# Selective-scan layer on one core: the low-order bfloat16 pieces of B formed by TensorE in PSUM instead of by GpSimd subtractions

## The chip, the cores and the metric

One core of one Trainium2 chip runs the whole program as one launch. The metric is the device time of a launch in microseconds. The kernel before took 12329.48 us, the median of three runs (12318.48, 12329.48 and 12333.17). A further run was profiled: it took 12328.75 us, of which 12326.7 us lie between its first and its last instruction.

## The reference, cut to what matters

Four layers run in sequence on x of shape (8, 64, 64, 64). Only the first, a vision state-space layer, is touched by the change. For each of 8 images, 128 channels d, 4 scan directions k and 16 states n it computes, along a sequence of 4096 pixels t:

```
x_dbl = einsum('bkdl,kcd->bkcl', xs, xproj_w)         # 4 + 16 + 16 rows: step sizes, B, C
dt    = softplus(dtproj(x_dbl[:4]) + dtproj_b)        # per channel d
h[d,n,t] = h[d,n,t-1] * exp(dt[d,t] * A[d,n]) + dt[d,t] * B[n,t] * u[d,t]
y[d,t]   = sum_n h[d,n,t] * C[n,t]
```

Directions 0 and 2 read the image by rows, forward and backward; 1 and 3 by columns. B[n,t] does not depend on the channel, so the kernel has to spread one row of B over 128 partitions for every state n.

## The kernel before, in words

**Units, steps and images.** `scan_layer` cuts a sequence into 4 chunks of `CH` = 1024 pixels. A chunk of one direction is a *step*, and a step has 16 *turns* n = 0 to 15, one for each state. Eight images of 16 steps make 2048 turns. Images 0 to 6 take the directions in the order 0, 2, 1, 3; the last image takes 1, 3, 0, 2. In this text step s = 0 is the first of the 16 steps of an image.

**What a turn does.** ScalarE writes a = exp(dt*A_n) (`decay`, L733). The row of B for the state is spread over the partitions in one of two ways: for n in `BY_POOL` = 0, 3, 6, 8 a broadcast DMA brings it as `bt`, GpSimd multiplies it by dt*u (`product`, L741) and ScalarE copies it to PSUM tile z (`spread`, L748); for the twelve other states TensorE spreads it into z with two 512-column bfloat16 matmuls against the 0/1 matrix `pick` (L751), and VectorE multiplies z by dt*u (L778). VectorE then runs the scan (`tensor_tensor_scan`, L782) into h, GpSimd multiplies h by the broadcast row of C (`ct`, L787), and TensorE adds the product into `yps` by an identity matmul (`sum_up`, L848), two to three turns later. h has three buffers, a three, z two, `ct` five and `bt` two.

**The three pieces of B.** The bfloat16 matmul would lose bits of B, so B is stored as three bfloat16 pieces stacked on 48 partitions, which `pick` adds up: p0 = bf16(B), p1 = bf16(B - p0), p2 = bf16(B - p0 - p1). The function `pieces` makes them once for each chunk and each pair of directions, that is in the step ahead of every step with k < 2. Its parts are hung on turns of the running step (`hooks`): `fetch` reads B (128x256 float32, tile `bw`) back from DRAM, `first` rounds it on ScalarE (L691), `subtract` forms the remainder `br` on GpSimd (L695), `second` rounds that on ScalarE (L698), `third` subtracts again on GpSimd (L701), `store` writes the three pieces with three DMAs (L706), and `get` reads them as `bs` (L713). In the general case these stand at turns 7, 8, 9, 10, 11, 12 and 13. For directions 2 and 3 only `get` is needed, at turn 13. I call the steps in which the pieces for the next step are made *parts steps*: 64 of the 128, four of which are at the start (made as the first image is being filled) and have another placement.

**What sets the order.** The order is written out by hand (`manual_schedule`): each engine runs its instructions strictly in program order. A queue of smaller items (`Background`: projections, normalization, convolution, output) gives one item to a turn, made by `bg.before` and finished by `bg.after` one turn later. In the turns listed in `idle` (6, 7, 8) only items without TensorE work may run. The two softplus activations of the next step stand at turns 6 and 7 (L653 and L656, the second with two table loads around it), its sum at turn 8 (L659), and dt*u of the next step at turn 11 (L678, GpSimd). At turn 3 `begin_sum` (L839) opens a new `yps` after ScalarE has emptied the last (L817).

**Normalization of y.** `norm_y` puts, among other items, eight `variance` items in the queue. Each one ends in `put`: ScalarE copies a row into `vrow` (L344), of which there is one buffer, and SyncE's queue sends it to DRAM (L345). Between some of the variance items stand items that only load (`load(at)`).

Of the kernel before, what the change touches and what calls it, by code (L numbers as in the profile page):

```python
# [11 lines left out]
BF16 = mybir.dt.bfloat16  # L12
AF = mybir.ActivationFunctionType
ALU = mybir.AluOpType
# [14 lines left out]
NCH = L // CH  # L29
# [212 lines left out]
def scan_layer(cm, x_in, w, xh):  # L242

    tc, nc = cm.tc, cm.nc
    with ExitStack() as ctx:
# [34 lines left out]
        for k in range(4):  # L280
# [5 lines left out]
            ps = psum.tile([128, BK], F32, name="wps", tag="mm")  # L286
# [31 lines left out]

        eps = cm.tile([128, 1], "eps")
        nc.vector.memset(eps, 1e-5)  # L320
        pick = cm.pool.tile([3 * N, N], BF16, name="pick", tag="pick")
        rows = work.tile([3 * N, N], F32, name="rows", tag="vsm")
        nc.vector.tensor_reduce(
# [7 lines left out]
        def bank(name):  # L331
            return psum.tile([128, BK], F32, name=name, tag="mm")
# [93 lines left out]
        def norm_y(y, blocks, load, multiply, project_out):  # L426

            put, chain, sm = inverse_root(len(blocks))
            j0, nb, sq = blocks[0], len(blocks), {}

            def square(j):
                sq[j] = work.tile([128, BK], F32, name="sq", tag="sq")
                nc.scalar.activation(sq[j], y[:, bass.ts(j, BK)], AF.Square)

            def variance(j):
                def make():
                    ps = bank("vps1")
                    nc.tensor.matmul(
                        ps[:1], lno_avg[:, NBK - 1 : NBK], sq.pop(j), start=True, stop=True
                    )  # L440
                    return ps

                def use(ps):
                    put(ps, 1, j - j0)
                    if j + 2 in blocks:
                        square(j + 2)

                return make, use

            def apply(j):  # L450
                def make():
                    ps = bank("rps")

                    row = cm.ident[:nb, j - j0 : j - j0 + 1].to_broadcast([nb, DI])
                    nc.tensor.matmul(ps, row, sm["r"], start=True, stop=True)
                    return ps

                def use(ps):
                    v = y[:, bass.ts(j, BK)]
                    nc.vector.tensor_tensor(v, v, ps, ALU.mult)  # L460
                    nc.scalar.activation(v, v, AF.Identity, bias=on_b, scale=on_g)
                    if j - 1 in blocks:
                        multiply(j - 1)

                return make, use

            out = [(None, lambda _: [square(j) for j in blocks[:2]]), none]
            for j in blocks:
                out.append(variance(j))
                if j in blocks[1:6:2] or nb == 2:  # L470
                    at = j if nb == 2 else j0 + (j - j0) // 2
                    out.append((None, lambda _, at=at: load(at)))
            out += chain
            out += [apply(j) for j in blocks[:2]]
            end = (None, lambda _: multiply(blocks[-1]))
            if nb == 2:
                out += [end, none]
            for j in blocks:
                if j + 2 in blocks:
                    out.append(apply(j + 2))  # L480
                    if j + 2 == blocks[-1]:
                        out.append(end)
                out += [project_out(j), none]
            return out
# [191 lines left out]
        def step_input(ctl):  # L676

            nc.gpsimd.tensor_tensor(ctl["dus"], ctl["dt"], ctl["ut"]["u"], ALU.mult)  # L678


        def pieces(ctl, low):

            by_place = "a n (j x) -> (n j) a x"

            def fetch():
                low["b"] = work.tile([128, 2, 128], F32, name="bw", tag="bw", bufs=1)
                nc.sync.dma_start(low["b"], low["bc"][:, :N].rearrange(by_place, x=128))

            def first():
                low["p"] = work.tile([128, 3, 2, 128], BF16, name="bp", tag="bp", bufs=1)  # L690
                nc.scalar.copy(low["p"][:, 0], low["b"])  # L691

            def subtract():
                low["r"] = work.tile([128, 2, 128], F32, name="br", tag="br", bufs=1)
                nc.gpsimd.tensor_tensor(low["r"], low["b"], low["p"][:, 0], ALU.subtract)  # L695

            def second():
                nc.scalar.copy(low["p"][:, 1], low["r"])  # L698

            def third():  # L700
                nc.gpsimd.tensor_tensor(low["p"][:, 2], low["r"], low["p"][:, 1], ALU.subtract)  # L701

            def store():
                low["bsd"] = dr.tile([2, 3 * N, CH], BF16, name="bsd", tag="bsd", bufs=8)
                for i in range(3):
                    nc.sync.dma_start(  # L706
                        low["bsd"][:, i * N : (i + 1) * N].rearrange(by_place, x=128),
                        low["p"][:, i],
                    )

            def get():
                ctl["bs"] = work.tile([3 * N, CH], BF16, name="bs", tag="bs")
                nc.sync.dma_start(ctl["bs"], low["bsd"][ctl["k"] // 2])  # L713

            return ([fetch, first, subtract, second, third, store] if ctl["k"] < 2 else []) + [get]


        BY_POOL = (0, 3, 6, 8)
# [5 lines left out]
        def load(ctl, n, t):  # L724

            bcr = ctl["bc"].rearrange("(t n) l -> t n l", t=2)
            name = "bt" if t == 0 else "ct"
            ctl[name, n] = bcp.tile([DI, CH], F32, name=name, tag=name, bufs=5 if t else 2)
            nc.sync.dma_start(ctl[name, n], bcr[t, n].unsqueeze(0).broadcast_to([DI, CH]))
# [128 lines left out]
        def steps(b):  # L858


            out = []
            for k in (0, 2, 1, 3) if b < NB - 1 else (1, 3, 0, 2):
                cs = range(NCH) if k < 2 else range(NCH - 1, -1, -1)
                out += [(k, c, i) for i, c in enumerate(cs)]
            return out
# [3 lines left out]
        def prepare(b, s):  # L869

            if b not in images:
                return None
            u = images[b]["u"]
            k, c, i = steps(b)[s]
            ks = [steps(b)[q * NCH][0] % 2 for q in range(4)] + [0]
            q = s // NCH
            bg.finish(b, 2 * c + 2 if s < NCH and k == 0 else NBK)
            low = lows.setdefault((b, k % 2, c), {}) if k < 2 else lows.pop((b, k % 2, c))
            dt, ut, e, items, soft = project(u, k, c, low)
            if b == 0 and s < NCH:  # L880
                items = later.pop(s, []) + items + [(None, soft[0]), (None, soft[1])]
            bg.add(items, first=True)
            new = work.tile([DI, N], F32, name="state", tag="state", bufs=3)
            ctl = dict(
                b=b, k=k, c=c, u=u, into=("row", "col")[ks[q + q % 2]], dt=dt, bc=low["bc"][k // 2], ut=ut, dus=e, soft=soft, new=new, state=None,
                first=(i == 0), new_y=(s < NCH), turns=(s % (2 * NCH) == NCH - 1),
                mat=lno_cen if s >= 3 * NCH - 1 else cm.ident,
            )
            ctl["pieces"] = pieces(ctl, low)
            return ctl  # L890


# [18 lines left out]
        with tc.manual_schedule():  # L911
            start(0)
            bg.drain()
            ctl = prepare(0, 0)
# [12 lines left out]
            for b in range(NB):  # L927
                for s in range(4 * NCH):


                    early, late = b == 0 and s + 1 < NCH, b == NB - 1 and s > 3 * NCH
                    if s + 1 < 4 * NCH:
                        nxt = prepare(b, s + 1)
                    else:
                        nxt = prepare(b + 1, 0)
                    bg.credit = 2 if b == NB - 2 else 1
                    idle = () if early or late else (6, 7, 8)
                    hooks = {}
                    if nxt:
                        do = nxt["pieces"]  # L940
                        if early:
                            hooks = {
                                12: [do[0]], 13: [nxt["soft"][2], lambda: step_input(nxt)] + do[1:5],
                                14: do[5:6], 15: do[6:],
                            }
                        else:
                            hooks = {14 - len(do) + i: [f] for i, f in enumerate(do)}
                            for i, f in zip((6, 7, 8), nxt["soft"]):
                                hooks[i] = hooks.get(i, []) + [f]
                            hooks[11] = hooks.get(11, []) + [lambda: step_input(nxt)]  # L950
# [51 lines left out]
                    ctl = nxt  # L1002
# [1155 lines left out]
```

## Time and profile before

| | |
|---|---|
| median of three runs | 12329.48 us |
| profiled execution | 12328.75 us, span 12326.7 us |
| TensorE busy | 11203.1 us (91%), 38827 matmul records |
| VectorE busy | 10359.2 us (84%) |
| ScalarE busy | 7820.8 us (63%) |
| GpSimd busy | 7399.3 us (60%) |
| scan layer | about 94 us to 7010 us of the span |
| GpSimd L695 and L701 | 43.1 and 43.2 us in all, 64 of each, 674 and 675 ns |
| ScalarE L691 and L698 | 25.6 and 25.9 us in all, 401 and 405 ns |

The busy shares are over the whole program. The scan layer fills a little over half of the span; the later layers hardly use GpSimd, so its share inside the scan layer is far higher than 60%. A time that a listing gives as "us" is the busy time of one instruction or of several merged ones ("x4"); the distance from one start to the next is often shorter than that, because the end of one overlaps the start of the next. An idle time is written in brackets with what ended it.

### The profile page before, as it was taken

The page shows a single profiled execution, that of the slowest core. Times are in us where ns is not written, and L with a number is a line of the kernel's source. Part 1 is how long each engine was busy: PE and PEld are TensorE (multiplying, and loading weights), DVE is VectorE, ACT ScalarE, POOL GpSimd, SP SyncE. Part 2 cuts the span into 40 slices and gives each one's busy share as a digit, 9 for nine tenths or more (in the row PEclk, how much of TensorE's full clock was granted, in tenths as well). Part 3 has the DMA queues.
Part 4 walks back from the last instruction along what each step waited for, and adds up shares of the span by engine and source line. Part 5 has one row for each costly group of instructions (what it writes and reads, how often), then busy time and mean ns, then how long its engine had stood idle before and what let it go on. Part 6 is the DMA issues. An engine that isn't in the chain of part 4 may idle for free. (4 is left out here: it accounts for less than half of the span.)

```text
span 12326.7 us, 120038 instructions
## 1 busy us (share of the span) xinstructions
PE 11203.1 (91%) x38827; PEld 4075.9 (33%) x38827; DVE 10359.2 (84%) x7334; ACT 7820.8 (63%) x10409; POOL 7399.3 (60%) x3510
## 2 busy tenths in 40 slices
PE   7899999999999999999998899999987779999999
PEld 2233332332332332333322233232335463333333
DVE  5999999999999999999999776868677686676767
ACT  4776776776766766767766554646547574555554
POOL 5999999999999999999999700000006480000000
PEclk8999999999999999999999899999998789999999
DMA  3666666666666666666666400000011100000000
GB/s 115 207 213 218 209 209 217 219 203 216 218 210 213 211 210 217 213 215 213 199 213 211 164 24 26 5 25 7 17 41 41 41 21 24 19 4 19 5 11 6
DMA packets 541331, 1562.16 MB, mean 127 GB/s; under 512 B 127360, under 2 KB 144400, under 8 KB 538128
## 3 DMA queue, kind: packets, MB, share of 16 engines
q1 hardware_dynamic: 540688, 1554.36, 38.5%
q8 instruction: 309, 5.06, 0.2%
q14 instruction: 334, 2.74, 0.1%
HBM read 1456.41 MB, written 88.87 MB: 125 GB/s over the span
## 5 line engine op out<-in xcount | busy, mean ns | idle before, releaser
L787 POOL TENSOR_TENSOR ct<-ct,h 128x1024 f32<-128x1024 f32 x2048 | 4794.6, 2364 | 248.2 <-DVE h L782 113.3
L782 DVE TENSOR_TENSOR_SCAN h<-a,state,z 128x1024 f32<-128x1024 f32 x1536 | 3573.1, 2342 | 118.2 <-ACT z L748 67.1
L1159 DVE TENSOR_TENSOR sum<-sum,ex 128x1024 f32<-128x1024 f32 x1920 | 2347.5, 1223 | 618.1 <-ACT ex L1152 484.4
L1152 ACT ACTIVATE ex<-sc 128x1024 f32<-128x1024 f32 x2048 | 1968.1, 1024 | 1359.6 <-PE sc L1147 1359.6
L848 PE MATMUL yps<-ct,ident 128*128 128x512 f32 x5632 | 2809.0, 630 | 2.5 <-POOL ct L787 2.4
L733 ACT ACTIVATE a<-dt,amat 128x1024 f32<-128x1024 f32 x2048 | 2345.4, 1147 | 725.9 <-DVE h L782 712.5
L778 DVE TENSOR_TENSOR z<-z,e 128x1024 f32<-128x1024 f32 x1536 | 1863.3, 1213 | 221.1 <-PE z L751 143.2
L1166 PE MATMUL av<-ex,v 128*64 128x512 f32 x8192 | 1950.0, 604 | 0.0
L1147 PE MATMUL sc<-q,k 16*128 16x512 f32 (+1 forms) x8192 | 1562.2, 623 | 4.2 <-ACT q L1140 3.1
L848 PEld LDWEIGHTS yps<-ct,ident 128*128 128x128 f32 x5632 | 1006.4, 194 | 1384.2 <-issue 1220.6
L751 PE MATMUL z<-bs,pick 48*128 48x512 bf16 x3072 | 948.0, 389 | 536.5 <-DVE h L782 485.5
L848 PE MATMUL yps<-ct,lno_cen 128*128 128x512 f32 x2560 | 1276.3, 630 | 0.0
L782 DVE TENSOR_TENSOR_SCAN h<-a,z 128x1024 f32<-128x1024 f32 x512 | 1162.7, 2282 | 81.4 <-ACT z L748 57.2
L741 POOL TENSOR_TENSOR bt<-bt,e 128x1024 f32<-128x1024 f32 x512 | 1210.1, 2364 | 5.3 <-DMA bt<-bc 5.3
L1473 POOL TENSOR_TENSOR gt<-gt,pad 128x1024 f32<-128x1024 f32 x16 | 34.9, 2179 | 1570.2 <-ACT gt L1472 1570.2
L1166 PEld LDWEIGHTS av<-ex,v 128*64 128x64 f32 x8192 | 512.2, 136 | 1332.8 <-issue 1278.9
L1147 PEld LDWEIGHTS sc<-q,k 16*128 16x128 f32 (+1 forms) x8192 | 528.4, 184 | 1016.2 <-issue 977.3
L748 ACT COPY z<-bt 128x1024 f32<-128x1024 f32 x512 | 519.8, 1015 | 537.5 <-POOL bt L741 334.8
L751 PEld LDWEIGHTS <-pick 48*128 48x128 bf16 x3072 | 177.6, 95 | 1754.9 <-DVE h L782 1003.0
L848 PEld LDWEIGHTS yps<-ct,lno_cen 128*128 128x128 f32 x2560 | 458.1, 193 | 618.3 <-issue 564.2
L544 PE MATMUL vps<-pad,convd 128*128 128x512 f32 x1152 | 550.9, 602 | 12.9 <-ACT e L648 12.9
L1846 DVE RECIPROCAL r<-e 128x512 f32<-128x512 f32 x128 | 420.7, 3323 | 0.0
(416 smaller groups left out, 10449.5 us busy)
## 6 DMA issues: line engine op xcount, KB each, us to landing
ct<-bc SPq DMA_DIRECT2D x2048, 512.0 KB
bt<-bc SPq DMA_DIRECT2D x512, 512.0 KB
x<-x SPq DMA_DIRECT2D x12, 2048.0 KB
bc<-e SPq DMA_DIRECT2D x128, 128.0 KB
zd<-z SPq DMA_DIRECT2D x64, 256.0 KB
z<-zd SPq DMA_DIRECT2D x64, 256.0 KB
x<-x SPq DMA_DIRECT2D x32, 512.0 KB
part<-x SPq DMA_DIRECT2D x128, 128.0 KB
```

What stands on the lines that cost most here:

```text
L544: nc.tensor.matmul(held[0].rearrange("p (r c) -> p r c", c=S), convd[:, t, :], pad[:, j * rows + dy : (j + 1) * rows + dy, dx : dx + S], s ...
L733: ctl["exp", n] = nc.scalar.activation(ctl["a", n], ctl["dt"], AF.Exp, scale=amat[:, ctl["k"], n : n + 1])
L741: nc.gpsimd.tensor_tensor(bt, bt, ctl["dus"], ALU.mult)
L751: nc.tensor.matmul(z[:, bass.ts(i, BK)], pick[:, n : n + 1].to_broadcast([3 * N, DI]), ctl["bs"][:, bass.ts(i, BK)], start=True, stop=True,)
L778: first = nc.vector.tensor_tensor(z, z, ctl["dus"], ALU.mult)
L782: nc.vector.tensor_tensor_scan(h[:, flip], a[:, flip], z[:, flip], 0.0 if state is None else state[:, n : n + 1], ALU.mult, ALU.add,)
L787: freed[at] = nc.gpsimd.tensor_tensor(ct, ct, h, ALU.mult)
L848: nc.tensor.matmul(ctl["ps"][:, bass.ts(i, BK)], ctl["mat"], ct[:, bass.ts(i, BK)], start=False, stop=(n == N - 1 and not ctl["turns"]),)
L1147: nc.tensor.matmul(sc[:, e, :], k[r : r + d, bass.ts(j, 128)], qs[i][r : r + d, :], start=True, stop=True,)
L1152: nc.scalar.activation(ex, sc, AF.Exp)
L1159: nc.vector.tensor_tensor(sums[i], sums[i], ex, ALU.add)
L1166: nc.tensor.matmul(avs[i][r, :], v[:, j, r], ex[:, e, :], start=(j == 0), stop=(j == TQ - 1))
```

## The change

`pieces` gets a second way to make p1 and p2, used everywhere but in the first four steps. `rest(i)` allocates a PSUM bank and lets TensorE form the remainder there: an identity matmul of the float32 B (256 columns), then one bfloat16 matmul with minus the identity (`minus`, a new constant) for each piece already there. ScalarE then rounds the PSUM result into piece i. So `rest(1)` has two matmuls and a ScalarE copy, `rest(2)` three matmuls and a ScalarE copy; the two GpSimd subtractions, the tile `br` and the ScalarE rounding of `br` go. In the parts steps the turns become: `fetch` 5 (was 7), `first` 7 (was 8), `rest(1)` 8, `rest(2)` 9, `store` 10 (was 12), `get` 13. Turn 9 joins the idle turns in parts steps. In `norm_y` the separate load items go; the first three variance items issue the loads themselves.

```diff
@@ scan_layer
+        minus = cm.pool.tile([128, 128], BF16, name="minus", tag="minus")
+        nc.vector.tensor_scalar(minus, cm.ident, -1.0, None, ALU.mult)
@@ norm_y
                     if j + 2 in blocks:
                         square(j + 2)
+                    if j - j0 < 3:
+                        load(j)
...
             for j in blocks:
                 out.append(variance(j))
-                if j in blocks[1:6:2] or nb == 2:
-                    at = j if nb == 2 else j0 + (j - j0) // 2
-                    out.append((None, lambda _, at=at: load(at)))
@@ pieces
-        def pieces(ctl, low):
+        def pieces(ctl, low, early):
...
-            return ([fetch, first, subtract, second, third, store] if ctl["k"] < 2 else []) + [get]
+            def rest(i):
+                def do():
+                    ps = bank("brps")
+                    b, p = (low[n] for n in "bp")
+                    nc.tensor.matmul(ps[:, :256], cm.ident, b.rearrange("p a x -> p (a x)"), start=True, stop=False)
+                    for q in range(i):
+                        nc.tensor.matmul(
+                            ps[:, :256], minus, p[:, q].rearrange("p a x -> p (a x)"),
+                            start=False, stop=(q == i - 1),
+                        )
+                    nc.scalar.copy(p[:, i].rearrange("p a x -> p (a x)"), ps[:, :256])
+
+                return do
+
+            if ctl["k"] >= 2:
+                return [get]
+            if early:
+                return [fetch, first, subtract, second, third, store, get]
+            return [fetch, first, rest(1), rest(2), store, get]
@@ prepare
-            ctl["pieces"] = pieces(ctl, low)
+            ctl["pieces"] = pieces(ctl, low, b == 0 and s < NCH)
@@ the main loop
-                    idle = () if early or late else (6, 7, 8)
+                    parts = nxt and not early and nxt["k"] < 2
+                    idle = () if early or late else (6, 7, 8, 9) if parts else (6, 7, 8)
...
-                            hooks = {14 - len(do) + i: [f] for i, f in enumerate(do)}
+                            hooks = dict(zip((5, 7, 8, 9, 10, 13) if parts else (13,), ([f] for f in do)))
                             for i, f in zip((6, 7, 8), nxt["soft"]):
                                 hooks[i] = hooks.get(i, []) + [f]
```

## The prediction

> **What bounds the kernel now.** I read the busy shares first, then the stretches of the scan layer, then the lists of instructions in order of time. [...]The windows show that layer in stretches of 1000 us (columns: stretch, its length, busy time and instructions of each engine, TensorE clock, DMA share, GB/s):
>
> ```profile
> 2000.00:3000.00 1000.00, 929.99 (x2123) 313.55 (x2122) 957.46 (x547) 705.74 (x1017) 979.57 (x444) 0.97 0.65 214
> 3000.00:4000.00 1000.00, 923.47 (x2119) 313.96 (x2117) 959.55 (x543) 717.95 (x1033) 978.52 (x440) 0.97 0.65 212
> ```
>
> GpSimd is busy 98%, VectorE 96%, TensorE 93%: three engines stand within 5% of each other, so the largest share decides nothing. The instructions at stake are small (groups; x64 each, 60 of them outside the first four steps):
>
> ```profile
> L701 POOL TENSOR_TENSOR bp<-br,bp 128x256 bf16<-128x256 f32 x64 | 43.2, 675 | 2.1 <-ACT bp L698 2.1
> L695 POOL TENSOR_TENSOR br<-bw,bp 128x256 f32<-128x256 f32 x64 | 43.1, 674 | 0.0
> L698 ACT CAST bp<-br 128x256 bf16<-128x256 f32 x64 | 25.9, 405 | 203.5 <-POOL br L695 203.3
> ```
>
> GpSimd's list for one parts step shows the queue without a gap, both subtractions in it:
>
> ```profile
> 3132.67 2.37 POOL L659 TENSOR_TENSOR dt<-dt,e 128x1024 f32<-128x1024 f32 x1
> 3134.99 2.35 POOL L787 TENSOR_TENSOR ct<-ct,h 128x1024 f32<-128x1024 f32 x1
> 3137.30 0.67 POOL L695 TENSOR_TENSOR br<-bw,bp 128x256 f32<-128x256 f32 x1
> 3137.93 4.68 POOL L787 TENSOR_TENSOR ct<-ct,h 128x1024 f32<-128x1024 f32 x2
> 3142.56 0.68 POOL L701 TENSOR_TENSOR bp<-br,bp 128x256 bf16<-128x256 f32 x1
> 3143.19 2.36 POOL L678 TENSOR_TENSOR e<-dt,ut 128x1024 f32<-128x1024 f32 x1
> ```
>
> From start to start a subtraction holds the queue 0.63 us, so 1.26 us a step. But TensorE is without a gap too where image 3 begins. Over 2726 to 2804 us the waits of TensorE and those of GpSimd are both empty lists; TensorE's list in that stretch runs on like this:
>
> ```profile
> 2757.02 1.98 PE L848 MATMUL yps<-ct,ident 128*128 128x512 f32 x4
> 2758.94 1.02 PE L438 MATMUL vps<-sq,lno_avg 128*1 128x512 f32 x2
> 2759.89 0.60 PE L751 MATMUL z<-bs,pick 48*128 48x512 bf16 x2
> 2760.42 1.98 PE L848 MATMUL yps<-ct,ident 128*128 128x512 f32 x4
> ```
>
> There, 52 us of step 0 hold 51.9 us of TensorE, 52.0 of GpSimd and 50.3 of VectorE. What ends the stretch is in ScalarE's list:
>
> ```profile
> 2797.03 0.17 ACT L769 COPY state<-h 128x1 f32<-128x1 f32 x1
> 2801.44 0.58 ACT L344 COPY vrow<-vps 1x512 f32<-1x512 f32 x1 [4.23 <-DMA vard<-vrow]
> ```
>
> ScalarE waits for a DMA that stands in SyncE's queue (issued at 2798.88) behind `ct` loads, which wait for TensorE to free a buffer; VectorE then stands still 3.4 us. The lateness of TensorE decides this stretch. In most other parts steps VectorE is without a gap from turn 9 on, at 3.50 us a turn, and TensorE waits for it: per step some 1.1, 1.3, 1.6, 1.6 and 1.1 us at turns 10 to 14 (waits of TensorE sorted by turn, over the 60 steps).
>
> To weigh this I walked back from the last scan of the layer, from each instruction to what released it last, as the page's chain does (the page's own reaches back only to 9143 us). The walk crosses one of the 120 subtractions only 15 times, in 14 steps. It runs through TensorE at turns 8 and 9 in 17 of the 60 steps: all seven of step 0 (images 1 to 7, the last leaving it at turn 9), four of step 1, four of step 9, two of step 10. Elsewhere it runs mostly through VectorE.
>
> **What the Trainium skill says.** "Perfetto Trace Analysis", Identifying the Most-Contended Engine: occupancy is a fair measure for Vector, Scalar and GpSimd, not for matmuls. It agrees for GpSimd; for TensorE I therefore use start-to-start times. "TensorE: Matmul & The Clock Gate", Back-to-back issue gap: 518 cycles for 512 columns, 262 for 256. Here a 512-column float32 matmul leaves two records with 0.43 us from start to start, as if each streamed twice; a bfloat16 one about 0.23 us. "ScalarE: Activation LUTs", What ACT_TABLE_LOAD costs: 186 ns + 0.833 ns per element, 399 ns for 256 elements, back-to-back ones overlapping by 93 ns. The trace has 401 and 405 ns, and 0.30 us from start to start (3132.41 to 3132.71 below).
>
> **The change part by part.**
>
> *GpSimd, removed:* 60 x 1.26 = 76 us of queue time. That is gain only where nothing else is as late. By the walk it is 15 x 0.63 = 9 us, or 14 x 1.26 = 18 us if both subtractions of a touched step count; I take 14. The ends are 9 and 76. What is late next is VectorE (50 to 52 us of a 52 to 53 us step) or TensorE.
>
> *TensorE, added:* the price is from the rows above. Two float32 records and the switch to them take 0.95 us (2758.94 to 2759.89), 0.86 of it streaming, so half the columns cost 0.43 + 0.10; a 256-column bfloat16 matmul 0.11 + 0.09. `rest(1)` is then 0.53 + 0.20 = 0.73, `rest(2)` 0.53 + 0.20 + 0.13 = 0.86 with the third matmul, 1.6 us a step. Below, bare streaming, 2 x 0.43 + 3 x 0.107 = 1.18; above, a switch of 0.2 us for each of the five matmuls, 2.2. No row shows a 256-column one, so these are estimates. It stands on the path in steps 0, 1 and 10: 13 x 1.6 = 21 us. In step 9 the order of instructions moves background work out, two gate projections of 0.95 us each, which pays for it. Elsewhere the waits at turns 10 to 14 (6.7 us together) cover it; without that cover it is 60 x 1.6 = 96 us. The background item of turn 9 moves to turn 10 or later, and in some steps one item passes to the next step; the sum of TensorE work stays, taken at nothing, from -5 to +5 us. Queued on TensorE behind `rest(2)`, which waits for ScalarE's p1, are the spreading of z for turn 11 and the sums. z is ready 2.3 us early in the median (lowest tenth 0.6), so this is taken at nothing, with an upper end of 10 us.
>
> *ScalarE:* `first` moves ahead of the softplus logarithm with its table loads; two PSUM copies stand at turns 8 and 9 in place of one copy from `br` at turn 10. The wait of 203 us for L695 goes, but behind it stand exponentials that are needed several microseconds later (at turn 12 they are 5.1 us early), so it gives nothing. The new order costs here:
>
> ```profile
> 3127.41 0.18 ACT L769 COPY state<-h 128x1 f32<-128x1 f32 x1
> 3127.61 1.28 ACT L656 ACT_TABLE_LOAD   x1
> 3128.90 1.06 ACT L656 ACTIVATE e<-e 128x1024 f32<-128x1024 f32 x1
> 3129.98 1.28 ACT L733 ACT_TABLE_LOAD   x1
> 3131.27 1.15 ACT L733 ACTIVATE a<-dt,amat 128x1024 f32<-128x1024 f32 x1
> 3132.33 0.17 ACT L769 COPY state<-h 128x1 f32<-128x1 f32 x1
> 3132.41 0.40 ACT L691 CAST bp<-bw 128x256 bf16<-128x256 f32 x1
> 3132.71 1.15 ACT L733 ACTIVATE a<-dt,amat 128x1024 f32<-128x1024 f32 x1
> ```
>
> The exponential that ends at 3132.42 is read by VectorE at 3132.64. Over the 60 steps it is 0.49 us early in the median, 0.17 in the lowest tenth. Putting 0.30 us before it costs something in a quarter to a third of the steps: 4 us; from 0 to 60 x 0.30 = 18.
>
> *SyncE's queue:* `fetch` passes the `ct` loads of turns 6 and 7; it waits until B has landed (3.6 us, by the wait of ScalarE on that DMA), which is nearly over by turn 5. The three stores pass the `ct` loads of turns 11 and 12 and a `bt` load, 0.4 us each, and no longer wait for GpSimd (141 us in all). Nothing either way; ends -5 and +10 us.
>
> *Normalization of y:* the load pairs go earlier, in `norm_y` alone. The variance items of turns 11 to 14 then follow each other without a load between, so ScalarE meets the wait for `vrow` four times an image instead of three, 4.3 us each (103.6 us over 24 times). At these turns the exponentials are 2.6 us early or more and ScalarE waits for GpSimd's `bt` anyway, so I take nothing; end 7 x 1.5 = 10 us. The new constant `minus` is one VectorE instruction, nothing.
>
> Sum: -14 + 21 + 4 = +11 us on the profiled execution's own 12328.75, so 12340. The median of the runs is 0.7 us above that execution, which makes no difference.
>
> **The rivals.** About 0.2% of 12329.5, 25 us, is what a measurement of this kernel can tell from no change; the three chances below use it.
>
> *No change that counts (0.50).* As worked out, 12340, own range 12315 to 12358.
>
> *GpSimd sets the pace (0.27).* In about half of the parts steps it has no gap for a whole step after the subtractions while VectorE has 0.6 to 1.7 us of gaps; if those come from GpSimd's lag, some 0.75 us a step is gained, 60 x 0.75 = 45: 12285; all of it would be 12253. Against it: GpSimd is idle 1.1 us in the average parts step, waiting for `ct` or h, and the walk passes it by.
>
> *TensorE is behind at turn 8 (0.20), slower.* Place: `rest(1)` and `rest(2)` before the z of turns 10 and 11. TensorE's waits at turns 8 and 9 are only 0.4 us a step each, so it barely catches up there. If half of the 60 steps are still behind and none catch up by turn 14: 30 x 1.6 = 48, + 4 - 10 = +42: 12371. It decides from about 20 steps on, where 20 x 1.6 outweighs GpSimd's gain.
>
> *The change moves nothing (0.03):* ScalarE's wait for GpSimd becomes one for TensorE of the same length, and the lag stays: 12329.
>
> **How the numbers follow.** Predicted 12340. The range goes to 12282, past the middle of the second case (about 0.12 left below), and to 12372, the middle of the third (about 0.08 above). Faster by over 0.2%: the second case, 0.27; slower: the third and 0.05 of the first, for the upper ends of ScalarE's and TensorE's costs, 0.25; within: the rest of the first and the fourth, 0.48.
>
> **What would show it.** In the profile after: L695 and L701 down to four each and GpSimd near 97% in the stretches above, more of its idle time waiting for h; step 0 longer by 1 to 2 us with TensorE without a wait; the other parts steps as long as before; two new matmul groups of some 1.6 us a step. I am wrong to the fast side if parts steps lose about 1 us each, to the slow side if VectorE waits for z at turns 10 and 11.

## The result and the profile after

The changed kernel takes 12352.07 us in the median of 20 runs (12327.8 to 12369.06), the kernel before 12332.27 us in 20 runs on the same chip. The ratio is 1.0017, with a 95% interval of 1.0011 to 1.0023: some 20 us slower, 14 to 28. That is inside the predicted range and within the 0.2% that was called no change, though here the measurement can just tell it from none. The profiled executions, one of each kernel, differ by 18.4 us (spans of 12345.1 and 12326.7 us), of which 19.9 lie between the first and the last scan of the scan layer.

The same two stretches of the scan layer in the kernel after (columns as before: stretch, length, busy time and instructions of TensorE, weight loads, VectorE, ScalarE, GpSimd, clock, DMA share, GB/s):

```profile
2000.00:3000.00 1000.00, 941.90 (x2170) 324.32 (x2171) 950.57 (x542) 707.04 (x1020) 962.09 (x423) 0.96 0.64 212
3000.00:4000.00 1000.00, 934.34 (x2170) 323.83 (x2169) 956.71 (x542) 718.58 (x1037) 966.23 (x421) 0.97 0.65 213
```

GpSimd falls from 97.9% to 96.4%, TensorE rises from 92.7% to 93.8%, and VectorE, which does the same work in both kernels, falls from 95.9% to 95.4%: it stands still longer. The freed GpSimd time was spent waiting. Over 260 to 6900 us GpSimd's C products waited 104.4 us for h and 114.9 us for the broadcast of C, where they waited 77.5 and 73.8 us before; the rise of 68 us stands against 76 us that were taken out.

The new instructions, from the list of the tile `brps` (duration as least/median/greatest ns, then first and last start), with what is left of the subtractions, from the list of the tile `bp`:

```profile
L720 PE MATMUL brps<-bw,ident x240: 379/379/634, 566.6 to 6739.0; 128*128 128x256 f32 x120
L722 PE MATMUL brps<-bp,minus x180: 269/272/421, 567.1 to 6739.3; 128*128 128x256 bf16 x180
L726 ACT CAST bp<-brps x120: 359/365/373, 570.1 to 6739.6; 128x256 bf16<-128x256 f32 x120
```

```profile
L696 POOL TENSOR_TENSOR br<-bw,bp x4: 667/667/668, 80.4 to 315.7; 128x256 f32<-128x256 f32 x4
```

The change does what it says. Its price is read from the starts in TensorE's list, here `rest(1)` of one parts step:

```profile
3142.96 0.59 PE L720 MATMUL brps<-bw,ident 128*128 128x256 f32 x2
3143.40 0.27 PE L722 MATMUL brps<-bp,minus 128*128 128x256 bf16 x1
3143.60 0.60 PE L770 MATMUL z<-bs,pick 48*128 48x512 bf16 x2
```

From 3142.96 to 3143.60 are 0.64 us; `rest(2)` takes 0.75 (both the medians of 60). That is 1.38 us a step, where 1.6 had been put.

**Where the time went.** I measure a step from its first scan to the next step's first scan, and sum over images 1 to 6, which take the directions in the same order (us, less the kernel before; the last column is the whole scan layer). Each row is one profiled execution, and executions of one kernel lie up to some 40 us apart (12327.8 to 12369.06 for the changed kernel), so small entries are not to be read:

| kernel | step 0 | step 1 | step 9 | step 11 | step 12 | scan layer |
|---|---|---|---|---|---|---|
| after | -10.2 | +11.4 | -14.2 | -18.0 | +33.1 | +19.9 |
| e1, turn 9 idle only | -0.2 | -21.3 | -8.4 | -16.8 | +34.4 | +20.2 |
| e3, no TensorE part | -8.5 | +6.1 | -14.2 | -21.3 | +32.1 | +17.5 |
| e4, idle 6, 8, 9 | +9.8 | +4.5 | +42.7 | -14.3 | +1.5 | +116.7 |
| e5, three empty items out | -10.1 | +13.3 | -7.5 | -14.6 | -2.4 | -7.3 |
| e10, two row buffers | -10.2 | -20.9 | -14.2 | -15.8 | +32.1 | -22.4 |
| e11, both | -10.0 | -20.6 | -8.6 | -13.0 | -3.2 | -61.3 |

Three things are seen at once: step 0, which I expected to become longer, is 1.7 us shorter each time; step 1 gives that back; and the largest loss is in step 12, about which the prediction says nothing: 5.6 to 8.2 us in each of images 1 to 5, nothing in image 6. The steps left out of the table are within 11 us of the kernel before in the changed kernel. In e1 they are not: its steps 3 to 5 lose 33.5 us, its step 1 gains 21.3, so only its step 12 can be set beside the changed kernel's.

**Step 0.** The window over step 0 of image 3, before and then after:

```profile
2724.90:2776.70 51.80, 51.63 (x123) 18.03 (x124) 50.08 (x29) 36.46 (x57) 51.80 (x25) 1.00 0.63 213
```

```profile
2737.34:2787.70 50.36, 50.22 (x124) 18.18 (x125) 49.75 (x29) 36.71 (x57) 50.23 (x23) 1.00 0.71 229
```

GpSimd has two instructions fewer. TensorE has seven new matmul records, yet only one more in all and 1.4 us less busy time: its list shows four convolution items of four matmul records (1.88 us of busy time each), where before a fifth and last one of two records (1.02 us) stood at the end of the step; three records of the sums also fall behind the step's end. With turn 9 closed to background items with TensorE work, that last item of the convolution went to the next step. Both engines that filled this step had less to do in it, and both were needed: e1 takes the item away and keeps the subtractions, and step 0 stays as it was (-0.2 us over the six images); e6 takes the subtractions away and keeps the item (-4.1); the changed kernel does both (-10.2).

Part of this is only put off. At turn 15 of step 0 the sum starts 11.6 us after the scan that it belongs to, where it was 9.6 before (means over the six images): TensorE goes into step 1 some 2 us further behind VectorE. What the matmuls would have cost with the item left in the step isn't settled. In e4, where turn 7 takes an item in place of turn 9, step 0 is 1.6 us longer each time (+9.8), but there it also begins with four sums that take 3.67 us instead of 1.98, after a wait of TensorE of 2.78 us.

**Step 1.** In the kernel after, ScalarE, SyncE's queue and VectorE in the same step of image 3:

```profile
2815.47 0.57 ACT L346 COPY vrow<-vps 1x512 f32<-1x512 f32 x1 [6.36 <-PE yps L867]
```

```profile
2812.03 0.32 SPq L748 DMA_DIRECT2D ct<-bc  x1
2812.78 0.23 SPq L347 DMA_DIRECT2D vard<-vrow  x1
```

```profile
2818.53 2.35 DVE L801 TENSOR_TENSOR_SCAN h<-a,state,z 128x1024 f32<-128x1024 f32 x1 [4.68 <-ACT z L767]
```

The profile names TensorE as what ScalarE waited for, but the copy overwrites the only `vrow`, whose last contents were sent to DRAM only at 2812.78, behind `ct` loads in SyncE's queue; the copy follows 2.69 us later, where in the kernel before, with the DMA named, it followed 2.56 us later (2798.88 to 2801.44). ScalarE's spreading of z stands behind this copy, and VectorE behind that: 4.68 us, where the same place cost 3.36 us before. e10 tests this reading.

**Step 12.** ScalarE in step 12 of image 3, after (the program runs exp as L752, the activation function Silu as L530 for a gate and L554 for a convolution):

```profile
3376.89 1.28 ACT L554 ACT_TABLE_LOAD   x1
...
3378.77 2.00 ACT L671 COPY ut<-u 128x1024 f32<-128x1024 f32 x1
3380.78 1.28 ACT L752 ACT_TABLE_LOAD   x1
...
3383.33 1.28 ACT L530 ACT_TABLE_LOAD   x1
...
3385.33 1.28 ACT L752 ACT_TABLE_LOAD   x1
3386.62 1.15 ACT L752 ACTIVATE a<-dt,amat 128x1024 f32<-128x1024 f32 x1
```

VectorE in the same stretch:

```profile
3383.40 1.23 DVE L797 TENSOR_TENSOR z<-z,e 128x1024 f32<-128x1024 f32 x1 [1.20 <-ACT state L788]
...
3389.22 2.29 DVE L801 TENSOR_TENSOR_SCAN h<-a,z 128x1024 f32<-128x1024 f32 x1 [2.26 <-ACT z L767]
```

Two background items that end in a Silu, a convolution and a gate, have slipped to both sides of the 2.0-us copy `ut`. I call these places turns 0 and 1 of step 12: a Silu is counted here at the turn whose exponential follows it in ScalarE's list, which is the turn after the one that issues it. Before, only `ut` stood there, and VectorE had one gap of 0.79 us in the whole step (of image 3). Each Silu between two exponentials costs two table loads. The Trainium skill's "ScalarE: Activation LUTs", What ACT_TABLE_LOAD costs, gives 1283 ns for the load and 1380 ns more to drain, 2.66 us for each switch. The trace agrees with the load and not with the drain: the exponentials on either side of the gate's Silu start 4.54 us apart (3382.08 and 3386.62), which is the exponential (1.05), the state copy (0.20), the Silu (0.71) and two loads (1.29 each), with nothing left over. So a Silu between exponentials costs ScalarE some 3.3 us. VectorE waits for z later in this step too (0.62 and 1.94 us). Here the Trainium skill's "TensorE: Matmul & The Clock Gate", HAM oscillation, bears on the case: it has the array's clock fall after waits of more than about 3.4 us. The trace agrees here; TensorE's convolution after a wait of 3.52 us takes twice the 1.88 us of the next one, and the clock granted from 3388 to 3394 us was 0.50:

```profile
3391.14 3.76 PE L545 MATMUL vps<-pad,convd 128*128 128x512 f32 x4 [3.52 <-ACT e L649]
```

Why the items slipped: closing turn 9 in the eight parts steps of an image takes eight turns from the queue, and what stands behind in it comes later. Whether the three load items that are gone give turns back can't be seen here: e1, which keeps them, has its Silus in the same turns. Turns of step 9 to 12 with a Silu, image 3, read from ScalarE's list (G gate, U convolution, turns counted as above; in these steps `ut` is copied at turn 0):

| kernel | step 9 | step 10 | step 11 | step 12 |
|---|---|---|---|---|
| before | 11G 13G 15G | 1U 11G 13G 15G | 1U 6G 11G 14U | 12U |
| after, e1 | 13G | 1U 12G 14G | 1U 6G 11G 13G 15G | 0U 1G 12U |
| e4 | 0G 1G 9G 13G 15G | 1U 9G 13G 15G | 1U 12U | 12U |
| e5 | 1G 12G 14G | 1U 12G 14G | 1U 6G 11G 13G 15U | 12U |
| e9 | 0G 1G 12G 14G | 1U 12G 14G | 1U 6G 11G 14U | 12U |

### The profile page after: what moved, and what is told of

Its sections match the earlier page's. It is cut to its first block, busy times and chain, and to the rows that moved or that the text cites. A ratio compares the mean times of both kernels' runs of the same rounds, so it can differ in the third digit from the quotient of the medians.

```text
span 12345.1 us, 120913 instructions
## 1 busy us (share of the span) xinstructions
PE 11262.9 (91%) x39247; PEld 4137.9 (34%) x39247; DVE 10356.2 (84%) x7335; ACT 7841.4 (64%) x10469; POOL 7327.8 (59%) x3390
## 5 line engine op out<-in xcount | busy, mean ns | idle before, releaser
L752 ACT ACTIVATE a<-dt,amat 128x1024 f32<-128x1024 f32 x2048 | 2347.5, 1147 | 894.5 <-DVE h L801 889.3
```

Of the source, the lines that this page charges most:

```text
L752: ctl["exp", n] = nc.scalar.activation(ctl["a", n], ctl["dt"], AF.Exp, scale=amat[:, ctl["k"], n : n + 1])
```

## The experiments

Every run was measured beside the kernel before, on different chips from one group of runs to the next, so I compare runs with each other by their ratios.

My theory after this comparison: the cost is in the order of ScalarE's background items, above all in step 12, and in step 1's wait for the row buffer, while the instructions that were removed and added nearly cancel. Rivals: the new matmuls cost the time (TensorE); or the earlier `first` and `fetch` do (ScalarE's order).

**e1: of the whole change, only turn 9 closed.** An edit of the kernel before:

```diff
-                    idle = () if early or late else (6, 7, 8)
+                    parts = nxt and not early and nxt["k"] < 2
+                    idle = () if early or late else (6, 7, 8, 9) if parts else (6, 7, 8)
```

> The kernel before with one edit: turn 9 is idle in parts steps, as in the changed kernel; the pieces are still made by GpSimd subtractions at their old turns. The theory formed from the two traces (background items slip): in the changed kernel the gate projections slip from step 11 into the first turns of step 12, where ScalarE loads tables for Silu and back four times beside the copy of u, and VectorE stands still some 6 us an image. The order of ScalarE's instructions slips the same way here, so this run should be slower than before by 15 to 40 us and show step 12 longer by 5 us or more. The prediction's theory (TensorE's added matmuls are what costs): moving background items costs nothing, within 5 us of before.

Measured: 12342.46 us against 12329.92, ratio 1.0013 (1.0006 to 1.0020), +12.5 us. By the ratio that is +16 us, from 7 to 25. There are no new matmuls in it and both subtractions are still there, yet step 12 loses 34.4 us over six images, as after. A closed turn that issues nothing is enough to make the kernel slower, and to make step 12 what it is after the change. The total is not that of the change less its other parts, though: step 1 is better here than after (-21.3 against +11.4), steps 3 to 5 are worse (+33.5 against -1.6).

**e2: no subtraction on GpSimd, nothing in its place.** An edit of the kernel before:

```diff
             def subtract():
-                low["r"] = work.tile([128, 2, 128], F32, name="br", tag="br", bufs=1)
-                nc.gpsimd.tensor_tensor(low["r"], low["b"], low["p"][:, 0], ALU.subtract)
+                pass
             def second():
-                nc.scalar.copy(low["p"][:, 1], low["r"])
+                nc.scalar.copy(low["p"][:, 1], low["b"])
             def third():
-                nc.gpsimd.tensor_tensor(low["p"][:, 2], low["r"], low["p"][:, 1], ALU.subtract)
+                pass
...
-                        low["p"][:, i],
+                        low["p"][:, min(i, 1)],
```

> The kernel before without the two GpSimd subtractions; ScalarE rounds B itself a second time at the same turn, and that piece is stored twice, so the low pieces of B are left out of the result. Nothing else moves. It measures what GpSimd's 1.26 us per parts step are worth alone. The prediction's theory: 9 to 18 us faster (0.07 to 0.15%). Rival, GpSimd sets the pace: 45 to 76 us faster (0.4 to 0.6%).

Measured: 12291.64 us against 12329.92, ratio 0.9974 (0.9964 to 0.9984), -38 us. About 17 us of that are gained before the fifth step of image 0, where the change doesn't touch the subtractions; so e6 was needed.

**e6: the same, only after the first four steps.** The edit of e2 under a condition that leaves the first four steps (`b == 0 and s < NCH`) as they were.

> As the run without subtractions, but the four parts steps of the start keep theirs, as they do in the changed kernel; the low pieces of B are left out of the result from there on. It measures the removal in just the 60 steps that the change touches. The profile of the run without any subtraction is 17 us shorter up to turn 0 of step 4, so some 20 us of its 38 should be left: theory (the start took half of that gain) 15 to 25 us faster than before, near the 9 to 18 of the prediction; rival, GpSimd's pace in the 60 steps: 38 us again.

Measured: 12312.84 us against 12332.1, ratio 0.9985 (0.9978 to 0.9992), -19 us. The prediction's term was -14. The rival in which GpSimd sets the pace needed -45 and is outside the interval (-27 to -10 us). ScalarE's wait for the remainder `br` goes in this run too, as it does in the change, so the 19 us are of both together.

**e3: the changed kernel without its five matmuls.**

```diff
                 def do():
-                    ps = bank("brps")
...
-                    nc.scalar.copy(p[:, i].rearrange("p a x -> p (a x)"), ps[:, :256])
+                    nc.scalar.copy(low["p"][:, i], low["b"])
```

> The changed kernel without the five TensorE matmuls of each parts step: ScalarE rounds B itself at turns 8 and 9, so the low pieces are left out of the result; the order of all else stays as in the changed kernel. The prediction's theory: 21 us faster than the changed kernel, that is about the time of before. Theory of the slip: the matmuls cost little, 0 to 8 us faster than the changed kernel, so still 12 to 20 us slower than before, with the long step 12 in it.

Measured: 12337.61 us against 12329.92, ratio 1.0008 (1.0001 to 1.0014). The changed kernel's 1.0017 less 1.0008 is 0.09%, 11 us for the matmuls; the medians of the two differ by 14, the profiled spans by 9. Each ratio is good to some 0.06%, so this is 11 with an error as large: the 21 us of the prediction are just inside it, the 48 us of the rival with TensorE behind are not. Of the steps, 0 and 1 show where the matmuls stand: with them step 0 is 1.7 us shorter and step 1 is 5.3 us longer over the six images than without (one profiled execution each). Step 12 keeps its loss without them.

**e8: `first` at turn 7 in the kernel before.** The hooks of the kernel before at turns 5, 7, 9, 10, 11, 12 and 13, so that `fetch` and `first` stand as in the changed kernel and the rest as it was:

```diff
-                            hooks = {14 - len(do) + i: [f] for i, f in enumerate(do)}
+                            hooks = dict(zip((5, 7, 9, 10, 11, 12, 13) if len(do) > 1 else (13,), ([f] for f in do)))
```

> The kernel before with the fetch of B at turn 5 and its first rounding at turn 7, ahead of the softplus logarithm, as in the changed kernel; all else at its old turn. It measures ScalarE's new order and the earlier fetch. The prediction's theory: 4 us slower than before, from 0 to 18. Rival, from the 16 us that the parts measured so far leave unexplained: 10 to 20 us slower.

Measured: 12343.57 us against 12332.1, ratio 1.0007 (0.9999 to 1.0015), about +9. The interval just reaches no change, so all that can be said is that it is not a gain and not over 18 us. The scan layer of its profiled execution is 7.6 us longer.

**e7: the loads of `norm_y` alone.** The change's edit of `norm_y` in the kernel before.

> The kernel before with the normalization's part of the change alone: no load items in the queue, the first three variance items load. The prediction took this at nothing with an end of +10 us. By the order of ScalarE's instructions a gate Silu then stands at turn 1 of step 9, and the variance rows follow each other more closely, so I now expect 0 to 15 us slower than before; if it is 0 within 5 us, this part has no share in the loss.

Measured: 12331.24 us against 12332.1, ratio 1.0001 (0.9992 to 1.0009). Nothing within some 10 us, as predicted.

**e4: turn 7 opened in place of turn 9.** An edit of the changed kernel that gives the queue its turns back:

```diff
-                    idle = () if early or late else (6, 7, 8, 9) if parts else (6, 7, 8)
+                    idle = () if early or late else (6, 8, 9) if parts else (6, 7, 8)
```

> The changed kernel with turn 7 open to background items in parts steps (idle turns 6, 8, 9), so that there are as many open turns as before; by the order of ScalarE's instructions the gate projections then end in step 11 at the latest and step 12 starts without them. Theory of the slip: step 12 loses its 5 to 6 us an image, 25 to 45 us faster than the changed kernel, 5 to 25 us faster than before. The prediction's theory: TensorE's work is the same, so within 5 us of the changed kernel, or slower, because a TensorE item now stands right ahead of the new matmuls.

Measured: 12432.75 us against 12329.92, ratio 1.0086 (1.0073 to 1.0099): 103 us slower. The expectation failed. Step 12 is clean (+1.5), but steps 9 and 10 lose 42.7 and 34.0 us: Silus now stand at turns 0 and 1 of step 9, and at turn 9 of both, which by the count used here is right ahead of `rest(1)`. TensorE's list in step 9 of image 3 shows what the last does:

```profile
3294.36 0.70 PE L720 MATMUL brps<-bw,ident 128*128 128x256 f32 x2 [2.92 <-ACT z L530]
...
3295.64 3.34 PE L867 MATMUL yps<-ct,ident 128*128 128x512 f32 x4
3298.76 0.98 PE L720 MATMUL brps<-bw,ident 128*128 128x256 f32 x2
```

In the changed kernel no remainder waits for a Silu; here one waits 2.92 us, presumably for the PSUM bank that the Silu still reads (not shown), and the z of the next turns stands behind it in TensorE's queue. After the wait four sums take 3.34 us instead of 1.98. VectorE waits for TensorE's z 209.3 us in all, against 124.2 in the changed kernel. So the place of the items can be worth far more than the instructions that the change adds or removes: this kernel has as many open turns as the kernel before.

**e5: three empty items out.** `norm_x` puts an empty item into the queue after each of four pairs of blocks. Taking three of the four out of the changed kernel moves the items behind them forward again:

```diff
-                if b:
+                if b and i == pairs[0]:
                     out.append(none)
```

> The changed kernel with three of the four empty items an image taken out of the queue behind the input projections, which gives back three of the turns that turn 9 took. By the order of ScalarE's instructions, step 12 then starts without a convolution or gate Silu, and one gate Silu stands at turn 1 of step 9 instead. Theory of the slip: the 5 to 6 us of step 12 go, at most 2 us come back in step 9, so 20 to 35 us faster than the changed kernel (12317 to 12332). The prediction's theory: nothing but TensorE's added work counts, so as the changed kernel, within 5 us.

Measured: 12316.92 us against 12332.1, ratio 0.9990 (0.9984 to 0.9997), 15 us faster than the kernel before. Against the changed kernel's ratio that is 0.27%, some 33 us. At the start of step 12 ScalarE's copy stands between two exponentials again, as before the change:

```profile
3349.99 2.00 ACT L671 COPY ut<-u 128x1024 f32<-128x1024 f32 x1
3351.89 1.15 ACT L752 ACTIVATE a<-dt,amat 128x1024 f32<-128x1024 f32 x1
```

There is no table load on either side of `ut`; step 12 is at -2.4 us, from +33.1, and step 9, where a gate now stands at turn 1, at -7.5, from -14.2. No engine's work has changed, since the items taken out were empty: all of this is place.

**e9: all four out.** `if False:` in place of the condition.

> As the run with three empty items taken out, but with all four out: step 12 is the same and clean, and step 9 now starts with two gate Silus at turns 0 and 1, beside the copy of u, the pattern that step 12 of the changed kernel has with a convolution Silu and a gate Silu. Theory that the place of the Silus decides (turns 0 and 1 cost 5 to 8 us an image): step 9 becomes 4 to 8 us longer than with three out, so 25 to 50 us slower than that run, about as the changed kernel. Rival, that only the number of open turns counts: as fast as with three out or a little faster.

Measured: 12341.86 us against 12328.48, ratio 1.0009 (1.0000 to 1.0017), 0.19% above e5 although the queue has one turn more. Step 12 is clean here too, but two gates stand at turns 0 and 1 of step 9, on either side of `ut`, and step 9 costs 17.9 us more than in e5 over the six images. So the place shows in step 9 as expected, and one more open turn did not help. That step 9 makes up the whole difference is not shown: the execution that was profiled, at 12322.68 us, is one of the two fastest of this run, and over the six images its other steps are together shorter than e5's by more than step 9 loses.

**e10: two row buffers.** The other loss, in step 1. An edit of the changed kernel:

```diff
-                t = work.tile([NBK, BK], F32, name="vrow", tag="rstd", bufs=1)
+                t = work.tile([2, BK], F32, name="vrow", tag="vrow", bufs=2)
```

The row also gets a tag of its own, where it shared its buffer with the tile `rstd`.

> The changed kernel with two buffers for the variance row in place of one shared with another tile. ScalarE's wait for the row's DMA (4.2 us in step 1, with VectorE standing still 4.7 us behind it) should go. Theory, that step 1 is as long as it is because of that wait: step 1 loses 3 to 5 us an image, 20 to 35 us faster than the changed kernel. Rival, that TensorE is as late itself in step 1: under 8 us.

Measured: 12306.28 us against 12328.48, ratio 0.9979 (0.9973 to 0.9986), some 46 us below the changed kernel by the ratios. Step 1 goes from +11.4 to -20.9 us, ScalarE's waits for `vard` fall from 93.4 to 3.0 us (over 260 to 6900 us), the 18.9 us of waits ahead of this copy that the profile puts down to TensorE's `yps` go as well, and step 12 keeps its loss (+32.1), as it should. (The wait of 4.2 us in the expectation is the one of the kernel before; here it was 6.36.) What the second buffer does and what the separate tag does was not taken apart.

**e11: both repairs.**

> The changed kernel with both repairs: three empty items out of the queue and two buffers for the variance row. If the two gains add up, 20 to 35 us faster than with the first repair alone, 12282 to 12297, faster than both kernels; if TensorE is what is late in step 1, as with the first repair alone.

Measured: 12259.96 us against 12328.48, ratio 0.9943 (0.9929 to 0.9956): 68.5 us faster than the kernel before, and the best version found. Below the changed kernel it is 0.74% by the ratios, where the two repairs one by one gave 0.27% and 0.38%: they add up, within the error.

**e12: two row buffers in the kernel before.** To see whether e10's gain belongs to the change at all.

> The kernel before with two buffers for the variance row and nothing else. It tells whether the change is worth having once that wait is gone. In before the stall of step 1 was 3.4 us where the changed kernel has 4.7, and three waits an image where it has four: so 24 to 46 us faster than before, 12283 to 12305. If it comes within 5 us of 12260, the best version owes nothing to the pieces made by TensorE; if it stays 20 us or more above, the change pays once its slipped items are put right.

Measured: 12311.34 us against 12324.06, ratio 0.9989 (0.9980 to 0.9997), -13 us. I had expected more. The waits of VectorE over 260 to 6900 us say where it went, before and then in e12 (total, times, longest):

```profile
DVE z L778 <- PE z L751: 117.2, 105, 6.1
DVE h L782 <- ACT z L748: 63.6, 33, 6.3
...
DVE h L782 <- POOL ct L787: 19.7, 30, 3.4
```

```profile
DVE z L778 <- PE z L751: 126.3, 108, 6.1
...
DVE h L782 <- POOL ct L787: 25.1, 38, 1.1
DVE h L782 <- ACT z L748: 22.7, 19, 6.3
```

The wait for ScalarE's z falls by 41 us, but the waits for TensorE's z and for GpSimd's `ct` rise by 14.5, and one for ScalarE's e (L628, not shown) by 8.3. Step 1 gets 26.9 us shorter over the six images, all steps together only 16.9. In the changed kernel the same repair takes 46 us from that wait (73.7 to 27.3) and the one for TensorE's z rises by 2.5 only. My reading is that without the change GpSimd is still full (98.3% of 2000 to 4000 us in e12), and what one wait gives up the next takes, while with it there is a little room (97.3% in e10). That rests on the lists; it wasn't tested by a further run.

## Why the prediction was right, and where its steps were not

The total was right (+11 predicted, +20 measured, 14 to 28), and so was the case that it named the likeliest. In part that was luck: what the background items cost was put at nothing, and a price of the matmuls that may be too high made up for some of it. By its own steps:

| step | predicted, us | measured alone, us |
|---|---|---|
| subtractions removed from GpSimd | -14 | -19 (e6) |
| matmuls on TensorE | +21 | about +11 (e3 against the changed kernel) |
| ScalarE's order, `first` and `fetch` earlier | +4 | about +9 (e8; interval reaches 0) |
| loads of `norm_y` | 0 | 0 (e7) |
| background items moved | 0 | about +16 (e1, 7 to 25, with other steps in it than after) |
| sum | +11 | about +17, against +20 in the whole |

*GpSimd.* Right in mechanism, and nearly in size. Crossings of the path counted with 0.6 to 1.3 us each gave a better value than the 76 us of busy time; the rest of those went into waits for h and for the broadcast of C.

*TensorE.* The mechanism, a price per step times the steps in which TensorE sets the end, gave about twice the middle of the measurement, whose error just takes it in. A smaller part of the difference is the price (1.38 us a step, not 1.6). The larger part is the place: step 0, half of the sum (7 of 13 steps), didn't get longer but shorter by 1.7 us. The prediction's sign of it, "step 0 longer by 1 to 2 us", was wrong: the item of turn 9 didn't stay in the step, and what TensorE was late by was carried into step 1.

*ScalarE.* Put at a quarter to a third of the steps; about twice that fits the measured value, whose error is as large as itself.

*Background items: the step that failed.* "[I]n some steps one item passes to the next step; the sum of TensorE work stays, taken at nothing, from -5 to +5 us." I saw two gate projections leave step 9 and counted TensorE's relief there (step 9 is 14.2 us shorter over six images), but didn't follow them to where they land. And an item has a second half on another engine, a Silu on ScalarE with two table loads; I followed only the half on TensorE. Where the Silus land on both sides of `ut` at turns 0 and 1 of step 12, VectorE stops: +33.1 us over six images, in a term that was put at -5 to +5. e1 shows the same loss from the closed turn alone, and e5 that with this meeting gone the change turns from 20 us of loss to 15 us of gain.

*The row buffer.* I named the wait for `vrow` in step 1, but expected it to be met more often at turns 11 to 14, where it does no harm. In image 3 it was met at turn 8 again, longer. e10 shows that a buffer which spares it is worth 46 us in the changed kernel.

*What was to be seen.* L695 down to four, GpSimd near 97% and waiting longer for h: seen. The matmul groups at 1.6 us: seen at 1.38. Step 0 longer: the opposite. Other parts steps as before: not so, as the table of steps shows.

*The rivals.* GpSimd setting the pace (12285) is ruled out by e6, TensorE behind at turn 8 in 30 steps (12371) by e3. The slower side came from neither.

Still open: the five terms leave some 3 us of the whole unexplained, which is within their errors, but e1's is not quite the change's; the split between steps 1 and 9 to 11 wasn't traced turn by turn (in image 6, steps 10 and 11 of the kernel before were some 7 and 9 us longer than in other images in its profiled execution, in the changed kernel 1 and 3, which flatters each of those columns by 5 to 6 us). And e11 is 0.46% below e12, some 57 us, but it also has three empty items fewer; the kernel before without those items was not tried, so how much of it the pieces on TensorE are worth by themselves is not settled.

## What to carry to other kernels

When an edit takes a slot from a queue that feeds a hand-written order, list every later item's new turn on each engine that it touches, not only on the engine for which the slot was closed: here the changed kernel with its queue's items in other turns lay anywhere from 15 us below to 103 us above the kernel before, and the arithmetic that had been moved was worth some 10 to 20. Where three engines stand within 5% of each other, what is freed on one may be worth a small part of its busy time, here about a quarter (19 of 76 us); the waits beside it can hold more (two small edits took the changed kernel from 0.17% above the kernel before to 0.57% below it). A single-buffered row that goes out by a shared DMA queue can make its writer wait for what stands ahead in that queue, as in step 1 here; the profile can name another engine for that wait, so look at when the buffer's last reader was issued.

## What the runs showed of the hardware

A 256-column float32 matmul (two records) and a bfloat16 one hold TensorE 0.64 us from start to start, where a pair of 512-column bfloat16 ones holds it 0.53. Waits of TensorE of 2.51 and 2.92 us (e4) and of 3.52 us (the changed kernel) were followed by matmuls at about half the speed (four records of 512 columns in 3.39 and 3.34 us instead of 1.98, and in 3.76 instead of 1.88). After the wait of 2.92 us that made 1.36 us on the sums and 0.39 on the remainder behind them. Not every wait of that length does it: after one of 2.49 us at 2725.04 in the kernel before, four sums took their 1.98. In the scan layer of the changed kernel, from the fifth step on, float32 matmuls came at reduced speed (512-column records over 0.7 us apart, where 0.43 is usual) within 6 us after 23 of 36 waits of 2.5 to 3 us, and after all nine of more than 3 us. Of a table switch between exponential and Silu, only the load of 1.28 us is seen.
